# A two-layer decoder on one core: layer 0's experts with the products of tokens and gates first in each part of a step, rotary on DVE, and more buffers for gated tokens in the last steps

## The chip, the cores and the metric

The kernel runs on one core of a Trainium2 chip. A core has five engines with a queue of instructions each: TensorE (PE, matmuls and transposes; its weight loads are shown apart as PEld), VectorE (DVE), ScalarE (ACT), GpSimd (POOL) and SyncE (SP), from which nearly all DMAs of the stage concerned are issued. An engine takes its instructions in order; one that waits holds up all behind it. The metric is the device time of one execution in microseconds (us). Of the kernel before, the median of three runs is 3584.25 us (3584.22 to 3586.48).

## The reference, cut to what matters

The whole computation is two decoder layers on x of 32 sequences of 100 tokens with 256 features, each layer with self-attention, cross-attention and a feed-forward part. The change touches only layer 0's feed-forward part, which is itself an attention with rotary followed by a choice of two experts out of eight. It gets the layer norm of x, and its result is added to x:

```python
q_in = _apply_rope(xh, sin, cos).reshape(B, S, E)   # r1 = x1*cos - x2*sin; r2 = x1*sin + x2*cos
q = (q_in @ Wq.T + bq).reshape(B, S, H, D)          # H = 16 heads of D = 16
k = (q_in @ Wk.T + bk).reshape(B, S, H, D)
v = (x @ Wv.T + bv).reshape(B, S, H, D)
...                                                 # causal attention, softmax
attn_out = ctx @ out_proj_w.T + out_proj_b
x1 = _layer_norm(x + attn_out, ln1_w, ln1_b)
gates = softmax(x1 @ gate_w.T + gate_b)             # 8 experts
_, top_idx = top_k(gates, 2)
expert_outputs = einsum('bsd,efd->bsef', x1, expert_w) + expert_b
...                                                 # the two chosen, times their gates, summed
return _layer_norm(x1 + moe_out, ln2_w, ln2_b)
```

Here S is 100, E (the width) is 256, and an expert is one 256x256 matrix with a bias.

## The kernel before, in words

**Tiling.** The 32 sequences form 8 groups of 4 (G = 4, NG = 8); a group has 400 tokens (GT), which stand either as rows (100 partitions, 4 sequences, 256 features) or turned (128 partitions, 2 halves of the features, 400 tokens). All is float32.

**The experts** are computed densely. A token's gate for an expert is zero unless the expert is one of its two. `gating(g, part)` (L985) makes the gates of group g: part 0 turns the rows x1 into x1T and multiplies by the gate weights; part 1 turns the logits back and takes exponentials; part 2 normalises and selects the top two (`top2`, L887), a chain of some twenty short DVE operations that ends in `wt`. `gates_turned` (L1026) turns `wt` on PE and stores it in DRAM; `gate(n)` (L1043) loads row n of it, broadcast to 128 partitions, into `wb` (three buffers), n counting group and expert, 0 to 63. `gated(n)` (L1053) multiplies the group's x1T by `wb` on DVE, one 128x800 product at L1056, into `xg` (two buffers). `experts(g, i, m)` (L1059) multiplies the gated tokens of experts 2i and 2i + 1 by the half m of their matrices on PE (L1068, each float32 matmul is two in the trace), the sum over experts running in PSUM for two and in `acc` on DVE for all (L1074); for i = 0 the biases are added on PE (L1063). `end(g, part)` (L1080) turns `acc` back (L1090), takes its layer norm, and adds it to x with three POOL operations (L1102 to L1104).

**The attention** (`heads_attention`, L275) is shared with layer 0's self-attention; the part that the change touches is its loop over steps. Here a step s is one sequence, g = s // 4 + 1 and i = s % 4. With 32 sequences there are 42 steps, 0 to 41; from step 32 on no attention work is left but the last output. `norm(g, part)` (L928) prepares a group: part 0 statistics on DVE (`stats`, L150, with its power on POOL at L174), part 1 scaling on ACT (L192), part 2 turns it on PE (L943), copies it on ACT (L946, `xlT`) and applies rotary: a product with cosines (L953, DVE for groups 0 and 1, POOL after), two products with sines on POOL (L955, `xwT`) and their sum on POOL (L958, `xrT`). `queries_or_keys` reads xrT, `values` reads xlT.

**The order** of PE, DVE, ACT and POOL is the program's own in this stage (`in_order`); buffers are handed out by the planner, and an instruction waits for the last reader of its buffer. In a step DVE's order is: `masked(s + 1, 0)` (L365), statistics of `norm` at i = 1, `fill(s, 0)`, `divided(s - 1)` (L423, L425), `lowered(s + 1, 0)` (L376, whose subtraction L377 is POOL's), `masked(s + 1, 1)`, `fill(s, 1)`, `lowered(s + 1, 1)`, `values` (L343), `fill(s, 2)`, `output(s - 1)` (L965), `fill(s, 3)`. PE's order is scores (L356), queries and keys (L223), the transposes of `norm`, `fill(s, 0)`, `divided` (L418), `turn_weights` (L389), `fill(s, 1)`, values, `turn_sums` (L431), `sums` (L405), `fill(s, 2)`, `output`, `fill(s, 3)`. PSUM has two double banks for scores and four single ones (`mm_tile`) for all else.

`fill(s, part)` (L1106) places the experts' work between the parts of a step. With 4i + part as the place in a group's four steps: `rows_of` (attention's residual and its layer norm) at 3, 4 and 6, `gating` at 9, 10 and 12, `gates_turned` at 14, all for the group before; `end` at i = 1. With n = 2(s - 9), `experts` for n and n + 1 stands in parts 1 and 2, and after all else comes the product n + 1 in part 0 and n + 2 in part 3, each followed by the load three ahead.

Of the kernel before, what the change touches and what calls it, by code (L numbers as in the profile page):

```python
# [10 lines left out]
F32 = mybir.dt.float32  # L11
# [4 lines left out]
ALU = mybir.AluOpType  # L16
AX = mybir.AxisListType

P = 128
B, T, D = 32, 100, 256  # L20
S2, DC = 361, 192
G = 4
NG = B // G
GT = G * T
H = 16
XH = 4
E = 8
# [39 lines left out]
def kernel(ctx: ExitStack, tc: tile.TileContext, io: dict, out: bass.AP):  # L67
    nc = tc.nc
# [49 lines left out]
    def bc(ap, axis, n):  # L118

        ap = ap.unsqueeze(axis)  # L120
        shape = list(ap.shape)
        shape[axis] = n
        return ap.to_broadcast(shape)
# [151 lines left out]
    def heads_attention(pool, w, wo, bias, norm, turn, res, fill):  # L275
# [87 lines left out]
        def masked(s, hf, ps):  # L363
            sm = pool.tile([T, 8, T], F32, tag="s", name="s", bufs=3)
            nc.vector.tensor_tensor(  # L365
                sm.rearrange("p (r j) k -> p r j k", r=2),
                ps[:T, :, :GT].rearrange("p r (j k) -> p r j k", k=T),
                bc(bc(causal, 1, 4), 1, 2), ALU.add,
            )
            sms[s, hf] = sm  # L370
# [74 lines left out]
            res(s, ps[:T, :D])  # L445

        with in_order():
            for part in range(3):
                norm(0, part)
            turned_[0] = turn(0)  # L450
            for m in range(4):
                queries_or_keys(0, m)
            values(0)
            ps = scores(0)
            for hf in range(2):
                masked(0, hf, ps[hf])
                lowered(0, hf)
                exponentials(0, hf)
            for part in range(3):
                norm(1, part)  # L460
            for s in range(B + 1 + fill.steps):
                g, i = s // G + 1, s % G
                more = s + 1 < B
                if more:
                    ps = scores(s + 1)
                    masked(s + 1, 0, ps[0])
                if g < NG:
                    if i == 0:
                        turned_[g] = turn(g)
                    for m in ((0,), (1,), (2, 3), ())[i]:  # L470
                        queries_or_keys(g, m)
                if i >= 1 and g + 1 < NG:
                    norm(g + 1, i - 1)
                fill(s, 0)
                if 1 <= s <= B:
                    divided(s - 1)
                if more:
                    lowered(s + 1, 0)
                    masked(s + 1, 1, ps[1])
                if s < B:  # L480
                    turn_weights(s)
                fill(s, 1)
                if more:
                    lowered(s + 1, 1)
                    values(s + 1)
                if 1 <= s <= B:
                    turn_sums(s - 1)
                if more:
                    exponentials(s + 1, 0)
                if s < B:  # L490
                    sums(s)
                fill(s, 2)
                if 1 <= s <= B:
                    output(s - 1)
                if more:
                    exponentials(s + 1, 1)
                fill(s, 3)
# [47 lines left out]
    rope = plain(w2, "rope", [P, 3, T])  # L545
    kch = CCH + [(S2, T)]
    NK = S2 + T
    with tc.tile_pool(name="x0", bufs=2) as pool, tc.tile_pool(name="x0p", bufs=1) as fixed:
# [288 lines left out]
        with in_order():  # L837
# [11 lines left out]
            for n in range(-4, B + 1):  # L849
# [14 lines left out]
                g = (n + 4) // G + 1  # L864
                if (n + 4) % G == 3 and g < NG:
                    lnTs[g] = latents_turned(lns.pop(g))
                g = (n + 5) // G
# [55 lines left out]
    with tc.tile_pool(name="f0", bufs=2) as pool:  # L923
# [4 lines left out]
        def norm(g, part):  # L928


            if part == 0:
                xls[g] = stats(xs[g], G, tag="n", shift=True)
            elif part == 1:
                xl = pool.tile([T, G, D], F32, tag="xl", name="xl", bufs=3)
                scaled(xl, xs[g], G, xls[g])
                xls[g] = xl
            else:
                xl2 = xls[g].rearrange("p g (d two) -> p g d two", two=2)
                xlT = xlTs[g] = pool.tile([P, 2, GT], F32, tag="xlT", name="xlT")
                for c in range(2):  # L940
                    ps = mm_tile()
                    for i in range(G):
                        nc.tensor.transpose(  # L943
                            ps[:, i * T : (i + 1) * T], xl2[:, i, :, c], ident[:T, :T]
                        )
                    nc.scalar.copy(xlT[:, c, :], ps[:, :GT])  # L946
                xrT = xrTs[g] = pool.tile([P, 2, GT], F32, tag="xrT", name="xrT")
                xwT = pool.tile([P, 2, GT], F32, tag="xwT", name="xwT", bufs=1)
                l4, r4, w4 = (
                    x.rearrange("p c (i t) -> p c i t", t=T) for x in (xlT, xrT, xwT)  # L950
                )
                first = nc.vector if g < 2 else nc.gpsimd
                first.tensor_tensor(r4, l4, bc(bc(rope[:, 0], 1, G), 1, 2), ALU.mult)  # L953
                for c in range(2):
                    nc.gpsimd.tensor_tensor(  # L955
                        w4[:, c], l4[:, 1 - c], bc(rope[:, 1 + c], 1, G), ALU.mult
                    )
                nc.gpsimd.tensor_tensor(xrT, xrT, xwT, ALU.add)  # L958

        def turn_group(g):  # L960
            return xrTs.pop(g), xlTs.pop(g)
# [81 lines left out]
        def gate(n):  # L1043

            if n < E * NG:
                g, e = n // E, n % E
                wb = pool.tile([P, GT], F32, tag="wb", name="wb", bufs=3)
                nc.sync.dma_start(
                    wb, wt_dram[g : g + 1, e * GT : (e + 1) * GT].to_broadcast([P, GT])
                )  # L1050
                wbs[n] = wb

        def gated(n):  # L1053
            if n < E * NG:
                xg = pool.tile([P, 2, GT], F32, tag="xg", name="xg")
                nc.vector.tensor_tensor(xg, x1Ts[n // E], bc(wbs.pop(n), 1, 2), ALU.mult)  # L1056
                xgs[n] = xg

# [47 lines left out]
        def fill(s, part):  # L1106

            g, i = s // G, s % G
            if 1 <= g <= NG:
                for at, f, *args in (  # L1110
                    (3, rows_of, 0), (4, rows_of, 1), (6, rows_of, 2), (9, gating, 0),
                    (10, gating, 1), (12, gating, 2), (14, gates_turned),
                ):
                    if 4 * i + part == at:
                        f(g - 1, *args)
                        if at == 14:
                            for n in range(3 if g == 1 else 1):
                                gate(E * (g - 1) + n)
            if 3 <= g and i == 1 and part in (0, 1, 3):
                end(g - 3, part)  # L1120


            n = 2 * (s - 2 * G - 1)
            if part in (1, 2) and 0 <= n < E * NG:
                experts(n // E, n % E // 2, part - 1)
            n += part // 3 + 1
            if part % 3 == 0 and 0 <= n < E * NG:
                gated(n)
                if n % E != 5:
                    gate(n + 3)  # L1130

        fill.steps = 2 * G + 1
        heads_attention(
# [311 lines left out]
    gated = {}  # L1445
# [840 lines left out]
```

## Time and profile before

| what | us |
|---|---|
| median of three runs | 3584.25 |
| the profiled execution | 3584.9 |
| its span | 3583.1 |
| PE busy | 3363.2 (94%) |
| DVE busy | 1863.4 (52%) |
| ACT busy | 1601.8 (45%) |
| POOL busy | 1287.8 (36%) |
| in 760 to 1365: PE, DVE, ACT, POOL busy | 509.43, 365.77, 235.41, 255.49 |
| L1056, products of tokens and gates, 64 | 69.1 (1089 ns each) |
| L953, L955, L958, rotary on POOL | 11.4, 17.7, 15.1 |
| L1068, experts' matmuls, 512 | 202.1 |

Times inside the execution are in us from the span's start. A row of the timeline gives start, duration, engine, line, operation, output and inputs, shape and count; in brackets stands how long the engine had been idle before and what ended that. Rows merge neighbours of one kind, so a row with x8 lasts from the first start to the last end. PE's clock is shown as a share of full speed.

### The profile page before, as it was taken

To read this page: it belongs to the slowest core of one execution; us is meant where nothing else is said; L and a number is where in the kernel's file an instruction comes from. 1 tells how busy PE (TensorE), PEld (TensorE's weight loads), DVE (VectorE), ACT (ScalarE), POOL (GpSimd) and SP (SyncE) were. 2 spreads that over 40 slices of the span, in tenths; PEclk is the share of its full clock that TensorE was granted. 3 is DMA by queue.
4 is the path that set the end of the run, shared out by engine and by line. 5 is a ranking of instruction groups with operands and counts; after the bars stand their busy time and mean duration, and the time that the engine had idled before them with its cause. 6 is when DMAs were issued, how large, how long until landed. Compare 5 with 4: busy or idle time off the path is not lost. (4 is left out here: it accounts for less than half of the span.)

```text
span 3583.1 us, 66359 instructions
## 1 busy us (share of the span) xinstructions
PE 3363.2 (94%) x25978; PEld 2261.1 (63%) x25978; DVE 1863.4 (52%) x5298; ACT 1601.8 (45%) x3533; POOL 1287.8 (36%) x947
## 2 busy tenths in 40 slices
PE   7998999968889977999999999999999999999997
PEld 5775666646556633333466666666666668899997
DVE  6777777636666644755455564555646552011111
ACT  4664666645434413566554544445444442211111
POOL 3445887855444421011133323333333332012221
PEclk9999999989999998999999999999999999999999
DMA  3002101000111111000100000000000003456665
GB/s 83 2 2 63 26 22 23 16 17 11 26 22 28 28 37 49 1 1 1 41 9 23 19 20 24 20 25 22 20 19 26 20 17 105 128 184 186 183 185 145
DMA packets 109218, 168.15 MB, mean 47 GB/s; under 512 B 14996, under 2 KB 89628, under 8 KB 108444
## 3 DMA queue, kind: packets, MB, share of 16 engines
q1 hardware_dynamic: 94238, 145.60, 13.6%
q0 software_dynamic: 12688, 15.36, 2.2%
q8 instruction: 207, 3.39, 0.4%
q10 hardware_dynamic: 1982, 2.95, 0.2%
q14 instruction: 103, 0.84, 0.1%
HBM read 138.32 MB, written 28.82 MB: 47 GB/s over the span
## 5 line engine op out<-in xcount | busy, mean ns | idle before, releaser
L1678 POOL TENSOR_TENSOR ex<-ex,rc 100x1444 f32<-100x1444 f32 x128 | 331.8, 2592 | 784.1 <-DVE rc L1677 742.8
L1669 ACT ACTIVATE ex<-s,nmx 100x361 f32<-100x361 f32 x512 | 303.2, 594 | 143.5 <-DVE nmx L1660 143.5
L377 POOL TENSOR_TENSOR s<-s,nmx 100x800 f32<-100x800 f32 x128 | 194.7, 1522 | 282.5 <-DVE nmx L376 206.3
L1276 ACT ACTIVATE h<-sc,cols 128x800 f32<-128x800 f32 x256 | 222.0, 924 | 134.9 <-PE sc L1270 134.5
L1660 DVE CUSTOM_DVE_ANT_0 s<-sc,mb 100x361 f32<-100x361 f32 x512 | 250.6, 527 | 7.6 <-PE sc L1653 7.6
L2133 POOL DMA_INDIRECT acc_dram<-y,xg x57 | 89.0, 1562 | 451.2 <-DVE y L2132 213.7
L1068 PE MATMUL mm<-xg,f_we 128*128 128x400 f32 x512 | 202.1, 537 | 39.6 <-DVE xg L1056 37.9
L2115 ACT ACTIVATE hgT<-sc 128x1024 f32<-128x1024 f32 x57 | 58.3, 1023 | 351.3 <-PE sc L223 351.3
L223 PE MATMUL sc<-xgT,w1b 128*128 128x128 f32 x1824 | 213.1, 275 | 0.4 <-DMA w1b<-in_f_w 0.4
L223 PEld LDWEIGHTS sc<-xgT,w1b 128*128 128x128 f32 x1824 | 208.3, 192 | 0.7 <-issue 0.6
L2132 DVE TENSOR_SCALAR y<-mm,gx 128x256 f32<-128x256 f32 x57 | 27.6, 484 | 348.1 <-PE mm L223 348.1
L223 PE MATMUL mm<-wx,hgT 128*128 x912 | 206.1, 380 | 0.0
L1653 PE MATMUL sc<-kT,qT 64*100 64x361 f32 x1024 | 197.8, 463 | 0.0
L1625 PE MATMUL mm<-x_wa,cT 128*128 128x512 f32 (+1 forms) x512 | 191.0, 496 | 0.1
L1685 PE MATMUL mm<-ident,ex 100*128 100x100 f32 (+1 forms) x1536 | 168.7, 258 | 18.7 <-ACT kT L1607 9.7
L174 POOL TENSOR_TENSOR rs<-va,neghalf 100x4 f32<-100x4 f32 (+1 forms) x96 | 97.5, 1018 | 237.1 <-DVE va L170 120.7
L223 PEld LDWEIGHTS mm<-wx,hgT 128*128 128x128 f32 x912 | 169.2, 190 | 20.5
L1703 PEld LDWEIGHTS mm<-eT,vb 128*64 128x64 f32 (+1 forms) x3072 | 136.8, 137 | 67.3 <-issue 66.4
L1595 PE MATMUL mm<-cT,x_wa 128*128 128x361 f32 x512 | 177.9, 470 | 0.7 <-DVE lnT L148 0.7
L1068 PEld LDWEIGHTS mm<-xg,f_we 128*128 128x128 f32 x512 | 96.5, 199 | 123.1 <-DVE xg L1056 46.1
L1685 PEld LDWEIGHTS mm<-ident,ex 100*128 100x128 f32 (+1 forms) x1536 | 143.1, 152 | 39.8 <-ACT kT L1607 13.9
L1692 ACT COPY eT<-mm 128x400 f32<-128x400 f32 (+1 forms) x256 | 125.6, 491 | 89.9 <-PE mm L1685 88.5
(347 smaller groups left out, 7323.6 us busy)
## 6 DMA issues: line engine op xcount, KB each, us to landing
w1b<-in_f_w SPq DMA_DIRECT2D x57, 1024.0 KB
wb<-wt_dram SPq DMA_DIRECT2D x64, 200.0 KB
wx<-in_f_w SPq DMA_DIRECT2D x8, 1024.0 KB
xg<-sorted_dram SPq DMA_DIRECT2D x57, 132.5 KB
cb<-in_ctx SPq DMA_DIRECT2D x32, 192.0 KB
cT<-in_ctxT SPq DMA_DIRECT2D x32, 180.5 KB
cT<-in_ctxT SPq DMA_DIRECT2D x64, 90.2 KB
x<-in_x SPq DMA_DIRECT2D x8, 400.0 KB
```

Source lines behind the costliest of these rows:

```text
L223: nc.tensor.matmul(ps, lhsT[k], rhs[k], start=(k == 0), stop=(k == n - 1))
L377: nc.gpsimd.tensor_tensor(sm, sm, bc(nmx, 2, T), ALU.add)
L1068: nc.tensor.matmul(ps[:, :GT], f0_we[:, k, e * D + m * P : e * D + (m + 1) * P], xgs[E * g + e][:, k, :], start=(i > 0 and e == 2 * i and ...
L1276: nc.scalar.activation(h1, both[r2][:, :, :GT], AF.Tanh, bias=col("a1_b1", o))
L1595: nc.tensor.matmul(kTs[u][c][:, :S2], x1_wa[:, m * P : (m + 1) * P], cT[:, 0, :], start=True, stop=False,)
L1625: nc.tensor.matmul(ps[e][:kn, :n], cT[:, 0, at], x1_wa[:, 1024 + c0 : 1024 + c0 + n], start=True, stop=False,)
L1653: nc.tensor.matmul(ps[:T, e, :S2], qT[p0 : p0 + 64, m, tok], kT[p0 : p0 + 64, c, :], start=True, stop=True,)
L1660: nc.vector.tensor_tensor_reduce(s[:, e, :], ps[:T, e, :S2], mb, 1.0, 3.4e38, ALU.add, ALU.min, nmx[:, e : e + 1],)
L1669: nc.scalar.activation(ex[:, 2 * c + e, :], s[:, e, :], AF.Exp, bias=nmx[:, e : e + 1], scale=-1.0, accum_out=sm[:, 2 * c + e : 2 * c + e ...
L1678: nc.gpsimd.tensor_tensor(ex, ex, bc(rc, 2, S2), ALU.mult)
L1685: nc.tensor.transpose(pt[:kn, j * T : (j + 1) * T], ex[:, j, k0 : k0 + kn], ident[:T, :T])
L1703: nc.tensor.matmul(po[64 * e : 64 * e + 64, m * T : (m + 1) * T], vb[k][:kn, v0 + 64 * h : v0 + 64 * h + 64] if k < 2 else vb[2 + u % 2][: ...
```

## The change

- `norm` gets a part 3: the rotary, taken out of part 2. All its four operations are on DVE, for every group. It is called after part 2 for groups 0 and 1, and for the others in the step with i = 3, after `masked(s + 1, 1)` and ahead of `turn_weights(s)`.
- In `fill`, the products stand first in parts 0 and 3, ahead of `rows_of`, `gating` and `end`. How far they go is counted: up to n + 1 in part 0 and n + 2 in part 3, as before; from step 32 on two more; until step 36 not past the last product of group 6 (number 55).
- The third part of `gating` (normalising and the top two) moves from place 12 (i = 3, part 0) to place 11 (i = 2, part 3).
- From product 48 on `xg` takes its buffers from the tags `xg`, `xlT` and `xrT` in turn, two products each: six buffers of one size.
- Loads of gates are issued in order by `gates()`, up to three ahead of the products made and as far as the gates have been stored.

```diff
@@ heads_attention
-            for part in range(3):
+            for part in range(4):
                 norm(0, part)
...
-            for part in range(3):
+            for part in range(4):
                 norm(1, part)
...
                     masked(s + 1, 1, ps[1])
+                if i == 3 and g + 1 < NG:
+                    norm(g + 1, 3)
                 if s < B:
                     turn_weights(s)
@@ norm
-            else:
+            elif part == 2:
                 xl2 = xls[g].rearrange("p g (d two) -> p g d two", two=2)
...
+            if part == 3:
+                xlT = xlTs[g]
                 xrT = xrTs[g] = pool.tile([P, 2, GT], F32, tag="xrT", name="xrT")
...
-                first = nc.vector if g < 2 else nc.gpsimd
-                first.tensor_tensor(r4, l4, bc(bc(rope[:, 0], 1, G), 1, 2), ALU.mult)
+                nc.vector.tensor_tensor(r4, l4, bc(bc(rope[:, 0], 1, G), 1, 2), ALU.mult)
                 for c in range(2):
-                    nc.gpsimd.tensor_tensor(
+                    nc.vector.tensor_tensor(
                         w4[:, c], l4[:, 1 - c], bc(rope[:, 1 + c], 1, G), ALU.mult
                     )
-                nc.gpsimd.tensor_tensor(xrT, xrT, xwT, ALU.add)
+                nc.vector.tensor_tensor(xrT, xrT, xwT, ALU.add)
@@ gated
-                xg = pool.tile([P, 2, GT], F32, tag="xg", name="xg")
+                tag = "xg" if n < 2 * (B - 2 * G) else ("xg", "xlT", "xrT")[(n // 2 + 1) % 3]
+                xg = pool.tile([P, 2, GT], F32, tag=tag, name="xg")
@@ fill
+            n = 2 * (s - 2 * G - 1)
+            if part % 3 == 0:
+                upto = n + part // 3 + 1
+                if s >= B:
+                    upto += 2
+                if s < B + G:
+                    upto = min(upto, E * (NG - 1) - 1)
+                while done[0] <= min(upto, loads[0] - 1):
+                    gated(done[0])
+                    done[0] += 1
+                    gates()
...
-                    (10, gating, 1), (12, gating, 2), (14, gates_turned),
+                    (10, gating, 1), (11, gating, 2), (14, gates_turned),
...
                         if at == 14:
-                            for n in range(3 if g == 1 else 1):
-                                gate(E * (g - 1) + n)
+                            stored[0] = E * g
+                            gates()
...
-            n += part // 3 + 1
-            if part % 3 == 0 and 0 <= n < E * NG:
-                gated(n)
-                if n % E != 5:
-                    gate(n + 3)
+
+        done, loads, stored = [0], [0], [0]
+
+        def gates():
+            while loads[0] < min(done[0] + 3, stored[0]):
+                gate(loads[0])
+                loads[0] += 1
```

More of the change, by code (lines that the diff above doesn't have):

```diff
@@ L1116, in fill @@
                         if at == 14:
-                            for n in range(3 if g == 1 else 1):
-                                gate(E * (g - 1) + n)
+                            stored[0] = E * g
+                            gates()
             if 3 <= g and i == 1 and part in (0, 1, 3):
                 end(g - 3, part)
-            n = 2 * (s - 2 * G - 1)
             if part in (1, 2) and 0 <= n < E * NG:
                 experts(n // E, n % E // 2, part - 1)
-            n += part // 3 + 1
-            if part % 3 == 0 and 0 <= n < E * NG:
-                gated(n)
-                if n % E != 5:
-                    gate(n + 3)
+        done, loads, stored = [0], [0], [0]
[3 more added lines that the diff above has]
+                loads[0] += 1
         fill.steps = 2 * G + 1
```

## The prediction

> **What bounds the kernel now.** I read the page first (PE 94% busy over the span), then busy times by stretch, which place the stage that the change touches: it begins near 760 us and its last transposes end at 1358. This answer is busy time of each engine per 40 us (PE, PEld, DVE, ACT, POOL), then PE's granted clock and DMA:
>
> ```profile
> 840.00:880.00 40.00, 31.81 (x357) 22.90 (x356) 27.24 (x68) 21.07 (x43) 20.17 (x22) 0.86 0.01 2
> 1160.00:1200.00 40.00, 38.32 (x322) 24.91 (x320) 27.23 (x67) 18.42 (x37) 20.46 (x16) 1.00 0.14 27
> 1280.00:1320.00 40.00, 30.47 (x77) 14.86 (x78) 17.19 (x46) 6.12 (x12) 9.93 (x7) 0.80 0.13 31
> ```
>
> PE is the bound in the middle, with DVE at two thirds; at the ends PE idles and its clock falls. So I listed PE's waits (total us, times, longest) in 760 to 1365:
>
> ```profile
> PE mm L1068 <- DVE xg L1056: 37.9, 16, 4.3
> PE mm L223 <- POOL xrT L958: 10.1, 3, 5.4
> ```
>
> Nearly all of PE's recoverable idle time is the wait for gated tokens. The timeline shows why, at step 11:
>
> ```profile
> 930.07 1.97 DVE L898 TENSOR_TENSOR hot<-rows,idf 100x32 f32<-100x32 f32 x2
> 932.07 1.87 POOL L958 TENSOR_TENSOR xrT<-xrT,xwT 128x800 f32<-128x800 f32 x1
> 932.07 1.91 DVE L1022 TENSOR_TENSOR wt<-hot 100x32 f32<-100x32 f32 x1
> 934.13 0.98 DVE L1056 TENSOR_TENSOR xg<-x1T,wb 128x800 f32<-128x800 f32 x1
> 935.16 3.03 PE L1068 MATMUL mm<-xg,f_we 128*128 128x400 f32 x4 [4.31 <-DVE xg L1056]
> ```
>
> The top-2 selection stands ahead of the product, and its small operations last as long as POOL's rotary operations beside them. At step 27, where no rotary is left:
>
> ```profile
> 1200.05 0.29 DVE L898 TENSOR_TENSOR hot<-rows,idf 100x32 f32<-100x32 f32 x2
> 1200.38 0.19 DVE L1022 TENSOR_TENSOR wt<-hot 100x32 f32<-100x32 f32 x1
> 1201.75 1.61 PE L1068 MATMUL mm<-xg,f_we 128*128 128x400 f32 x4 [1.78 <-DVE xg L1056]
> ```
>
> Same selection, 3.4 us shorter; the wait is 1.78, and the four matmuls take 1.61, not 3.03: after the long wait PE was at half clock. The last steps look like this:
>
> ```profile
> 1342.26 0.57 DVE L1074 TENSOR_TENSOR acc<-mm,acc 128x400 f32<-128x400 f32 x1 [2.11 <-PE mm L1068]
> 1342.75 1.88 DVE L1056 TENSOR_TENSOR xg<-x1T,wb 128x800 f32<-128x800 f32 x2
> 1343.79 5.64 PE L1068 MATMUL mm<-xg,f_we 128*128 128x400 f32 x16 [1.57 <-DVE xg L1056]
> ```
>
> PE and DVE take turns: with two buffers the next products can't start before PE is done with the last.
>
> [...]the 0.29 us pair takes 1.97 beside POOL.[...] Here waits over 4 us are followed by half-rate matmuls (3.03 for 1.61) and waits of 1.8 and 1.9 us are not; but 2.25 us at 1309.18, soon after another, is.[...]
>
> **The change, part by part.**
>
> *Rotary to DVE.* DVE gains per group two 128x400 products and a 128x800 sum, and from group 2 on the 128x800 product: 0.99 (its own row, L953 on DVE), twice 0.57, 0.98: 3.1 us. No row has a 128x400 with both operands in SBUF; 0.50 (half of 0.99) to 0.57 (the PSUM form, L1074) bound it, I take 0.57. That is 22.7 us on DVE in eight groups and 44.2 off POOL (11.4 + 17.7 + 15.1). For groups 0 and 1 the chain is bare, PE waits 5.42 and 3.85: POOL needed 4.8 us from turned tokens to xrT (769.35 to 774.15), DVE needs 3.1: saved 1.7 twice, **3.4**. At step 3 POOL's rotary holds back L377, so exponentials and PE (0.85, 1.15, 0.92): the first stays, the rest goes, with some clock: **2.5** (0 to 2.9).
>
> In a step with i = 3 the rotary now stands between the second mask and `turn_weights` in program order, after `divided`. Behind it on DVE wait the sum L1074, which frees a PSUM bank, the second maximum L376 (POOL's L377, ACT's exponential) and the values L343. At step 11, counting from 925.83: product to 926.8, top-2 to 929.8, mask 930.7, product 931.7, reciprocal and division 932.3, maximum 933.2, mask 934.1; [...]the rotary runs to 937.6 (start to start 2.8), sum 938.1, maximum 939.0, values 939.4. PE, with 1.1 us of wait, is through this step's experts at 938.6, wants the sum's bank then (free at 938.1), the values' bank at 940.4 and the exponentials (941.5) about 942.9. The cover is 0.5 us at the tightest; gone, each us of lateness would cost one.
>
> *Top-2 one part earlier.* DVE does the same work before the second product in either order: product, mask, top-2, product or product, top-2, mask, product. So this alone gains nothing; the gain is that POOL's rotary is no longer beside it. Steps 11, 15, 19, 23: waits of 4.31, 4.28, 4.13, 4.12 become 1.1 each (931.7 against PE ready at 930.6), 12.4 us. Half clock: 1.42 on the four matmuls, 0.88 on the values, 0.4 on what follows, 2.7 a time; half of that at step 23: 9.5. Together **21.9**. Step 7: the same selection delays the division, PE waits 4.42 (L431 at 877.94) and then runs slow (1.56 for 0.89, 1.76 for 1.03): the division moves from 877.8 to 873.8, PE wants it at 873.5: 4.1 + 3.1 = **7.2**. Steps 27 and 31 (1.78, 1.91): nothing.
>
> *Products first.* At i = 1 the product overtakes the statistics of `rows_of` (2.4 us): 0.91 at step 9, 0.80 at step 29, some 0.1 between: **2.0**. The statistics come one product (0.95) later, and ACT's scaling two parts on has room for that; the division doesn't move, both stood ahead of it. Each product is followed by one broadcast load, the same 64 in the same order; SP's queue holds only these and eight stores, so none is moved past another.
>
> *Six buffers, last steps.* From output(31) at 1272.14 to the last transpose at 1358.27 are 86.1 us. PE's work there: eight steps of experts at 5.5 (16 matmuls, 5.64 less the overlap), 44.0; biases 4 x 0.86; transposes and gating 0.9 + 0.9 + 1.24 + 0.85 + 1.45 + 0.3 + 0.9; output 0.86: 54.8. Waits left: group 7's own chain. L965 at 1273.6, POOL's sum 3.0[...], statistics 2.4, power 1.2, ACT 2.07: PE is there 0.9 us early; L148 stands behind two products: 1.8; top-2 behind a product: 2.0 before L1030; L1090 twice 0.6: together 5.9. So 60.7 us, 25.4 saved; three products instead of two ahead of the division at step 32 cost 0.5, a half-clock spell after such a wait about 1: **24.0**. Broadcasts: store to load issue is 1.4 us (1313.75 to 1315.18), three loads are down some 5 us after issue; group 7's first product isn't needed before step 37, one step of 5.5 us later than its load can land.
>
> Sum 3.4 + 2.5 + 21.9 + 7.2 + 2.0 + 24.0 = 61.0. The profiled execution took 3584.9 (span 3583.1 and 1.8 around it): 3523.9. The median of the runs is 0.65 lower, so 3523. What follows the stage starts as much earlier; no wait in it is for a fixed time.
>
> **Rivals.** (1) DVE becomes the bound at i = 3: half a us of cover isn't there, the sum's bank is late by some 2 us and half clock stays in steps 11 to 23. Then of 24.4 (steps 3 to 23, less step 7) about 5 is left: 3543.[...] Against: the count above. (2) The last steps gain half:[...] 3535. Against: one step of look-ahead is longer than that. (3) Slower: [...]the second exponentials arrive late and PE's `turn_weights` stalls at half clock, in all six steps of groups 2 to 7. It must eat 61 us and 7 more to be seen: over 11 us a step, where DVE's rotary and one L377 are 4.6 together. It would need every such step's delay to be handed on to the next two. (4) The products don't go ahead: the extra buffers are only taken from product 48 on, and if a slot of `xlT` or `xrT` were still held, the last steps would be as now: 3547. The last reader of `xlT` is values(31) at step 30, product 48 comes at step 32; unlikely.
>
> **How the numbers follow.** 0.2% is 7.2 us, about what a measurement tells from no change. The forecast 0.70 (own range 3513 to 3534: [...]4 for half-clock spells, 4 for the last steps), rival 1 0.11, rival 2 0.10, rival 4 0.03, slower 0.04, no change 0.02. Range 3511 to 3546: 0.70 less its own tail of 0.08, with most of rivals 1 and 2. Faster 0.94, same 0.02, slower 0.04.
>
> **What would show it.** PE's wait for L1056 falls from 37.9 us to under 12; the `hot` pair takes 0.3 everywhere; xrT is ready 3.1 us after xlT in groups 0 and 1; no POOL rotary; DVE near 1870 us busy (1863.4 + 22.7[...]); steps 37 to 40 run at 5.5 us. I am wrong if L1068, L389 or L223 wait for L1074 or the exponentials at i = 3, if half clock stays there, or if the stage shrinks and a later one grows.

## The result, and the profile after

| | before | after |
|---|---|---|
| median, us | 3584.23 (3582.7 to 3586.48, 6 runs) | 3557.18 (3556.24 to 3562.76, 6 runs) |
| span of the profiled execution | 3583.1 | 3554.4 |
| PE, DVE, ACT, POOL busy | 3363.2, 1863.4, 1601.8, 1287.8 | 3353.6, 1873.7, 1602.8, 1258.7 |

The changed kernel takes 0.9925 of the time (95% interval 0.9915 to 0.9936), 27 us less. The forecast was 61 us less, 3523 with a range of 3511 to 3546: the sign was right, the size was not, and the measurement lies above the range.

Busy time by stretch, after (length, then PE, PEld, DVE, ACT and POOL busy, PE's granted clock, DMA):

```profile
840.00:880.00 40.00, 33.32 (x408) 24.45 (x407) 29.16 (x75) 22.18 (x45) 16.68 (x17) 0.96 0.01 2
1280.00:1320.00 40.00, 37.55 (x117) 20.36 (x116) 24.26 (x53) 3.86 (x8) 11.68 (x7) 0.95 0.14 42
```

The last steps improved most (PE 37.55 of 40 for 30.47). PE's waits from 755 to 1335, after (total us, times, longest):

```profile
PE mm L1073 <- ACT back L410: 11.2, 4, 2.8
...
PE mm L1073 <- DVE xg L1061: 8.1, 7, 1.9
PE mm L223 <- DVE xrT L961: 7.2, 3, 3.6
```

The line numbers moved: L1073 is the experts' matmul (L1068 before), L1061 the product (L1056), L961 the rotary's last sum (L958). The wait for gated tokens fell from 37.9 us in 16 waits to 8.1 in 7. At the top stands a wait that wasn't there before: four times 2.8 us for `back`, ACT's copy of the attention's sums (L410). It means that PE has no PSUM bank: the experts' second half gets the bank that `back` still has to be copied out of. The timeline of step 11, after, shows what holds `back` up:

```profile
926.96 0.98 DVE L365 TENSOR_TENSOR s<-sc,causal 100x800 f32<-100x800 f32 x1
927.19 4.00 POOL L377 TENSOR_TENSOR s<-s,nmx 100x800 f32<-100x800 f32 x1 [10.48 <-DVE nmx L376]
927.86 0.98 DVE L956 TENSOR_TENSOR xrT<-xlT,rope 128x800 f32<-128x800 f32 x1
928.76 1.05 DVE L958 TENSOR_TENSOR xwT<-xlT,rope 128x400 f32<-128x400 f32 x2
929.84 2.19 DVE L961 TENSOR_TENSOR xrT<-xrT,xwT 128x800 f32<-128x800 f32 x1
931.22 0.87 ACT L382 ACTIVATE ex<-s 100x800 f32<-100x800 f32 x1 [2.63 <-POOL s L377]
932.00 0.47 ACT L410 COPY back<-mm 128x400 f32<-128x400 f32 x1
932.52 4.54 PE L1073 MATMUL mm<-xg,f_we 128*128 128x400 f32 x8 [2.81 <-ACT back L410]
```

Read it from below. PE waits 2.81 us for `back` and then runs in part at half clock (4.54 us for eight matmuls that take 2.95 in experiment 1; the granted clock over them is 0.64). `back` stands on ACT behind the first exponential (L382), which waits for POOL's L377: the sums that `back` copies were ready at 929.06, where PE's L405 ended, and it starts at 932.00. L377 is recorded as starting at 927.19, 0.67 us before the rotary, and takes 1.52 in experiments 1 and 9; here it takes 4.00 and ends at 931.19, 1.35 after the recorded start of the rotary's last operation, which lasts 2.19 for 0.98. The rotary's three products meanwhile last 0.98 and, the two together, 1.05, as they do in groups 0 and 1 with no L377 beside them (0.99 and 1.05). My estimate from these rows: L377's last 1.52 us begin at 929.67, about where the products end (929.81), so that it ran behind the products and the sum behind it. The same holds in all six steps with a rotary: L377 starts 0.67 to 0.74 us ahead of it and takes 4.00 to 4.07.

In the last steps the alternation of PE and DVE is gone, but three places are left, of which these rows show two (the third, 1.89 us for `wt`, was in the forecast):

```profile
1255.33 0.99 DVE L1061 TENSOR_TENSOR xg<-x1T,wb 128x800 f32<-128x800 f32 x1 [1.17 <-DMA wb<-wt_dram]
...
1257.00 0.39 PE L431 MATMUL mm<-ident,o 100*128 100x100 f32 x2 [1.58 <-DVE o L425]
...
1273.22 2.07 ACT L192 ACTIVATE yo<-yo,sh,rs 100x256 f32<-100x256 f32 x4 [1.84 <-POOL sh L176]
1275.20 0.67 ACT L139 ACTIVATE x1T<-mm,cols 128x400 f32<-128x400 f32 x1
...
1275.92 3.03 PE L223 MATMUL mm<-x1T,f_wg 128*128 128x400 f32 x4 [3.83 <-ACT x1T L139]
...
1307.16 19.07 PE L1073 MATMUL mm<-xg,f_we 128*128 128x400 f32 x56
```

At step 32 the third product of the three waits for its load, and the division behind it on DVE is late. At step 34 ACT's copy of x1T stands behind the scaling of `yo`, PE waits 3.83 us and falls to half clock (granted 0.50; 3.03 us for four matmuls that took 1.61 at 1201.75 of the kernel before, granted 1.00). From 1307 on the matmuls follow each other with no wait, as forecast.

**Where the time went, step by step.** PE's product of `oT` with `f_wo`, the start of each output, marks the steps. Differences of the marks, us (the last line ends with the last transposes):

| stretch | before | after | saved | forecast |
|---|---|---|---|---|
| span's start to output(0) | 814.25 | 811.70 | 2.55 | 3.4 |
| to output(4), rotary of step 3 in it | 37.07 | 39.03 | -1.96 | 2.5 |
| output(4) to (7), step 7 in it | 38.16 | 33.81 | 4.35 | 7.2 |
| to outputs 8, 12, 16, 20, 24, 28 (i = 1) | 96.73 | 93.74 | 2.99 | 2.0 |
| to outputs 10, 14, 18, 22 (steps 11 to 23) | 79.97 | 73.74 | 6.23 | 21.9 |
| to output(31), step 32 | 8.18 | 9.98 | -1.80 | part of 24.0 |
| output(31) to the last transposes | 86.13 | 67.93 | 18.20 | with the line above 24.0 |

With 0.16 lost in the other stretches the sum is 30.4 us. After the stage 1.7 us are lost again; nothing of the change is there, and no run tells where from. Single executions of one kernel differ by more than that (3538.33 to 3545.39 in experiment 12), and the profile is of one: no edit below changes an instruction ahead of the stage, yet its first transposes (L943, later L945) start anywhere from 763.95 us (experiment 12) to 770.40 (experiment 2), at 766.47 before and 767.85 after. So the first line of the table holds 1.38 us lost ahead of the stage and 3.93 saved in it.

### The profile page after: what moved, and what is told of

Same layout as the page of the kernel before. It is cut to its first block, busy times and chain, and to the rows that moved or that the text cites. A ratio compares the mean times of both kernels' runs of the same rounds, so it can differ in the third digit from the quotient of the medians.

```text
span 3554.4 us, 66360 instructions
## 1 busy us (share of the span) xinstructions
PE 3353.6 (94%) x25978; PEld 2256.7 (63%) x25978; DVE 1873.7 (53%) x5328; ACT 1602.8 (45%) x3533; POOL 1258.7 (35%) x917
## 3 DMA queue, kind: packets, MB, share of 16 engines
q10 hardware_dynamic: 1982, 2.95, 0.2%
## 5 line engine op out<-in xcount | busy, mean ns | idle before, releaser
L377 POOL TENSOR_TENSOR s<-s,nmx 100x800 f32<-100x800 f32 x128 | 210.1, 1641 | 332.4 <-DVE nmx L376 251.1
L1073 PE MATMUL mm<-xg,f_we 128*128 128x400 f32 x512 | 195.2, 527 | 19.3 <-ACT back L410 11.2
L1721 PE MATMUL mm<-eT,vb 128*64 128x100 f32 (+1 forms) x3072 | 162.3, 254 | 0.0
```

What stands on the lines that cost most here:

```text
L377: nc.gpsimd.tensor_tensor(sm, sm, bc(nmx, 2, T), ALU.add)
L1073: nc.tensor.matmul(ps[:, :GT], f0_we[:, k, e * D + m * P : e * D + (m + 1) * P], xgs[E * g + e][:, k, :], start=(i > 0 and e == 2 * i and ...
L1721: nc.tensor.matmul(po[64 * e : 64 * e + 64, m * T : (m + 1) * T], vb[k][:kn, v0 + 64 * h : v0 + 64 * h + 64] if k < 2 else vb[2 + u % 2][: ...
```

## The experiments

Each was compared with the kernel before on the same chip, where its median was between 3583.77 and 3586.98 us, so that ratios are the safer thing to compare; rows are from one execution each. The edits are to the changed kernel unless it is said otherwise. "Steps 11 to 23" is the stretch to outputs 10, 14, 18 and 22: 79.97 us before, 73.74 after.

**1. The rotary behind the values.**

```diff
-                if i == 3 and g + 1 < NG:
-                    norm(g + 1, 3)
                 if s < B:
                     turn_weights(s)
                 fill(s, 1)
                 if more:
                     lowered(s + 1, 1)
                     values(s + 1)
+                if i == 3 and g + 1 < NG:
+                    norm(g + 1, 3)
```

> The rotary of groups 2 to 7 stays on DVE but moves behind `values(s + 1)`, so that the division, both masks, both maxima and the values are ahead of it. Theory A ([...]L377 takes 4.0 us for 1.5, the first exponential and `back` behind it on ACT are late, and PE waits 2.81 us for `back`'s PSUM bank in steps 11, 15, 19, 23 and then runs at half clock): these four waits vanish and 4 x (2.8 + about 2.5) = 21 us are saved, with 3 to 5 more at steps 3 and 7: 3531 to 3537 against 3557 for the change. The long L377 is then the second half's, which nobody needs before the next step. Theory B (the 22.7 us added to DVE are what holds PE, wherever they stand): within 6 us of 3557, PE's waits moved to another bank or to the products.

Measured 3546.23 (3544.45 to 3548.76), ratio 0.9895 (0.9878 to 0.9911). Rows of step 11:

```profile
924.08 1.52 POOL L377 TENSOR_TENSOR s<-s,nmx 100x800 f32<-100x800 f32 x1 [10.48 <-DVE nmx L376]
...
926.35 3.44 POOL L377 TENSOR_TENSOR s<-s,nmx 100x800 f32<-100x800 f32 x1 [0.74 <-DVE nmx L376]
926.41 0.47 ACT L410 COPY back<-mm 128x400 f32<-128x400 f32 x1
926.54 2.95 PE L1073 MATMUL mm<-xg,f_we 128*128 128x400 f32 x8
```

The first L377 is back at 1.52, `back` is copied in time, PE doesn't wait and stays at full rate (2.95 us for the eight matmuls). Now the second L377 meets the rotary (3.44), and nothing waits for that. Steps 11 to 23 take 56.47 us, 17.3 less than in the changed kernel and 23.5 less than before: the place of the rotary was what cost the main term of the forecast. But the kernel gained 11 us only. The steps after these show where some of it went: outputs 9, 17, 29 and 30 come 20.36, 20.44, 19.50 and 13.97 us after their forerunners, for 18.76, 18.76, 16.52 and 12.36, with the same waits and half-rate matmuls after them. That is taken up below. The time lies between the two forecasts: theory A had the waits right and the total 9 to 15 us too low.

**2. `back` ahead of the first exponential,** in this stage alone (the one with a `bias`).

```diff
-                if more:
+                if bias is None and more:
                     exponentials(s + 1, 0)
                 if s < B:
                     sums(s)
+                if bias is not None and more:
+                    exponentials(s + 1, 0)
```

> The rotary stays where the change put it; in this stage ACT copies the weighted sums (`back`) ahead of the first half's exponential instead of behind it. Theory A: [...]`back` no longer stands behind it, so PE's wait for the bank in steps 11 to 23 goes: 15 to 21 us saved, 3536 to 3542. Theory B: no more than 5 us. If [...]the late second exponential is what counts, PE waits at L389 in the next step instead and less than half is saved.

Measured 3549.21 (3545.22 to 3553.65), ratio 0.9898 (0.9882 to 0.9915). The wait for `back` is gone with the rotary where the change put it and L377 still slow (4.00 us): steps 11 to 23 take 57.04 us. So it is `back` behind the exponential, not the exponential itself, that PE missed. The forecast of 3536 to 3542 was missed by the same kind of long stretches (output(17) 20.45, output(29) 19.55).

**3. Rotary back on POOL, all else as changed.** The four operations of groups 2 to 7 and the last three of groups 0 and 1, at the place they had before.

> The rotary of groups 2 to 7 is back on POOL in part 0 (and its last three operations of groups 0 and 1 too), all else as in the change. Theory A: the top-2 selection now starts some 2 us earlier than POOL's rotary[...]: a wait of 2 to 4 us for the product in steps 11 to 23; the last steps keep their gain: 3558 to 3568. Theory B: DVE is relieved of 22.7 us, PE's wait for the bank goes and nothing takes its place: under 3545.

Measured 3570.94 (3569.36 to 3571.33), ratio 0.9960 (0.9946 to 0.9975), 3 us above theory A: with the rest of the change in place, putting the rotary back on POOL costs half of the gain. PE's waits:

```profile
PE mm L1074 <- DVE xg L1062: 25.0, 7, 5.2
```

Steps 11 to 23 take 83.20 us, more than before the change: the selection, a part earlier, stands ahead of the step's second product, and its small operations still last as long as POOL's rotary beside them: at 930.98 one on `wt` takes 1.91 us beside POOL's 1.87, for 0.19 at 926.38 in experiment 4, with no POOL operation beside it.

**4. The selection back at place 12, all else as changed.**

```diff
-                    (10, gating, 1), (11, gating, 2), (14, gates_turned),
+                    (10, gating, 1), (12, gating, 2), (14, gates_turned),
```

> The changed kernel with the top-2 selection back at place 12 (i = 3, part 0), all else as changed. The prediction's step: its place alone gains nothing: 3555 to 3559. Rival (what counts is not the product but what stands behind the selection on DVE: division, maximum, POOL's subtraction, the first exponential, `back`): in the steps with i = 3 these are 2 to 3 us later, PE's wait for `back` grows from 2.8 to 4 to 6 us, and the wait of 0.83 for the product goes: four to six steps at 1.5 to 3 us: 3562 to 3575.

Measured 3561.26 (3560.54 to 3562.32), ratio 0.9935 (0.9918 to 0.9952), 4 us slower by the medians than with the early selection (the intervals overlap, but steps 11 to 23 are longer too, 76.61 us), just short of what the rival said and outside of what the forecast's step said. PE's first row of waits shows the term:

```profile
PE mm L1073 <- ACT back L410: 15.6, 4, 3.9
```

The product goes ahead of the selection, but division, maximum, L377 and `back` come later. In steps 27 and 31, where there is no rotary, the late place is the better one: output(26) follows in 12.94 us for 14.12, output(30) in 11.65 for 12.36.

**5. Products first alone, on the kernel before.** The block of the product and its load moved to the top of `fill`, nothing else.

> The kernel before with one part of the change alone: the products stand first in parts 0 and 3 of `fill`, as far as before and with the same loads behind them; rotary, selection and buffers as before. The prediction's step gives this 2.0 us, in the steps with i = 1: 3580 to 3583.5. Rival (in the last steps the order of the products is worth the 8 us that the changed kernel without products ahead kept there): 3573 to 3578, with output(31) to the last transposes at 78 us for 86.1.

Measured 3565.96 (3565.12 to 3570.1), ratio 0.9947 (0.9931 to 0.9964): 20 us from what the forecast priced at 2.0, and more than the rival gave it. Step 11 of this kernel:

```profile
926.13 0.98 DVE L1056 TENSOR_TENSOR xg<-x1T,wb 128x800 f32<-128x800 f32 x1
...
930.90 1.97 DVE L898 TENSOR_TENSOR hot<-rows,idf 100x32 f32<-100x32 f32 x2
...
934.10 0.36 PE L431 MATMUL mm<-ident,o 100*128 100x100 f32 x2 [2.54 <-DVE o L425]
```

With the product in front of the selection the wait of 4.31 for it is gone, though beside POOL's rotary the `hot` pair still lasts 1.97 (0.29 at step 27 of the kernel before); what is late is the division, by 2.54. Steps 11 to 23 take 69.15 us. From output(31) to the last transposes it is 79.2 us for 86.1: at step 33 the product no longer stands behind the statistics, where it made PE wait 3.76 us before.

With this run there are four kernels that all have the products first and differ, up to step 31, only in where the rotary and the selection stand. Steps 11 to 23 take:

| | selection late (place 12) | selection early (place 11) |
|---|---|---|
| rotary on POOL | 69.15 (experiment 5) | 83.20 (experiment 3) |
| rotary on DVE, ahead of `turn_weights` | 76.61 (experiment 4) | 73.74 (changed kernel) |

With the products first the old places of rotary and selection are the best of the four: each of the two moves alone makes these steps longer, and both together still by 4.6 us. Only once PE no longer waits for what stands behind L377 (56.47, 57.04 and 57.88 us, experiments 1, 2 and 9) is the rotary better on DVE.

**6. No products ahead, two buffers throughout.**

```diff
-                tag = "xg" if n < 2 * (B - 2 * G) else ("xg", "xlT", "xrT")[(n // 2 + 1) % 3]
+                tag = "xg"
@@ fill
-                if s >= B:
-                    upto += 2
```

> The change without the two products more from step 32 on and with two buffers throughout. The forecast had 24 us for this part; by the two traces it is 16 to 18: 3573 to 3576. If the last steps are bound by something else, 3560 to 3565.

Measured 3564.94 (3559.78 to 3566.4), ratio 0.9943 (0.9927 to 0.9960): products ahead are worth 8 us, half of the 16 to 18 that were expected of them. From output(31) to the last transposes it is 77.8 us, so 8.3 of the 18.2 saved there come without them, from the order.

**7. The two places of the last steps.**

```diff
-                if s >= B:
+                if s > B or (s == B and part == 3):
                     upto += 2
@@
-            if 3 <= g and i == 1 and part in (0, 1, 3):
+            if 3 <= g and i == 1 and part in (0, 1):
                 end(g - 3, part)
+            if 3 <= g and part == 3 and i == (3 if g == NG else 1):
+                end(g - 3, part)
```

> The changed kernel with the two edits of the last steps alone. Theory (the division at step 32 is late by a product that waits for its load, and x1T by the scaling of `yo`): the wait of the turn of o falls from 1.58 to under 0.3, that for x1T from 3.83 to 1.7, since DVE's half of x1T is ready at 1273.7, and the half-rate matmuls after it (3.03 and 3.73) go to full rate: 1.5 + 2.1 + 2.2 = 5.8 us, 3550 to 3553. Rival[...]: 3555 to 3559, with products of 3 us and more in steps 35 to 37.

Measured 3554.11 (3552.85 to 3556.97), ratio 0.9913 (0.9896 to 0.9929). The median is 3 us lower, not 5.8, and the profiled execution doesn't show where: from output(30) to the last transposes it takes 79.55 us, where the changed kernel's takes 77.91. Rows of it:

```profile
1270.47 0.31 PE L210 MATMUL mm<-ident,x 100*128 100x100 f32 x1 [2.25 <-ACT x L192]
...
1293.86 5.74 DVE L1061 TENSOR_TENSOR xg<-x1T,wb 128x800 f32<-128x800 f32 x2 [0.39 <-DMA wb<-wt_dram]
...
1303.04 5.65 PE L1073 MATMUL mm<-xg,f_we 128*128 128x400 f32 x8
```

The wait of 1.58 for the division is gone, and so is that of 3.83 for x1T. But three products now stand together at step 32, POOL's sum `xl` beside them (L979) takes 4.83 us for 3.93, and PE waits 2.25 for `x`, where it waited 0.63; the matmuls after it still run at half rate (3.03 and 3.75). Later it is as the rival said: POOL's operations of `end`, now at step 35, make two products last 5.74 us for 1.89, PE waits 1.90 for the sum into `acc` behind them, and half rate follows (5.65 for 2.95).

**8. Edits 1, 2 and 7 together.**

> The rotary moved behind the values and `back` ahead of the first exponential (both as in the two runs that had one of them), and in the last steps: no products ahead in part 0 of step 32, and in group 8's steps the scaling of `yo` moved from i = 1 to i = 3, so that ACT's copy of x1T isn't behind it. Theory: the gains add up where they are in different steps. 3546.2 with the late rotary, less 1.6 for the division at step 32, less 2.1 for the wait for x1T and 2.2 for the half clock behind it; the second of the first two edits adds at most 1. So 3539 to 3543. Rival[...]: 3544 to 3550, with half-rate matmuls in places where the kernel with the late rotary has full rate.

Measured 3547.76 (3545.89 to 3551.65), ratio 0.9898 (0.9882 to 0.9915), as the rival had it: the gains don't add up. From output(30) to the last transposes it takes 77.99 us for 78.27 in experiment 1, so the edits of the last steps bring next to nothing there. Steps 11 to 23 are as short as in the first experiment, and its long stretches are all there too (outputs 9, 17, 29 and 30 in 20.41, 20.45, 19.55 and 13.96).

**9. A pause ahead of the rotary.** For groups 2 to 7 a useless maximum, one input, 0.56 us:

```diff
+                if g >= 2:
+                    nc.vector.tensor_reduce(
+                        small.tile([P, 1], F32, tag="gap", name="gap"), xlT[:, 0, :], AX.X, ALU.max
+                    )
                 nc.vector.tensor_tensor(r4, l4, bc(bc(rope[:, 0], 1, G), 1, 2), ALU.mult)
```

> The changed kernel with a useless DVE operation of one input (a maximum over 128x400, some 0.5 us) ahead of the rotary for groups 2 to 7. In the changed kernel POOL's L377 starts at 927.19 and the rotary at 927.86, yet L377 lasts 4.00. Theory S[...]: with the pause L377 lasts 1.5 to 1.7, the rotary's first product 1.2 to 1.6, PE's wait for `back` falls from 2.8 to under 0.7 and full clock stays: 3543 to 3550. Theory D[...]: L377 lasts 4 us and more, the wait for `back` is 2.8 to 3.4: 3556 to 3561.

Measured 3541.51 (3538.93 to 3543.01), ratio 0.9880 (0.9864 to 0.9897). Work was added, and 16 us are gained, 1.5 more than theory S allowed for. Step 11 (here L1077 is the experts' matmul, L960 the rotary's first product):

```profile
925.19 1.52 POOL L377 TENSOR_TENSOR s<-s,nmx 100x800 f32<-100x800 f32 x1 [10.47 <-DVE nmx L376]
925.86 0.56 DVE L957 TENSOR_REDUCE gap<-xlT 128x1 f32<-128x400 f32 x1
...
926.33 1.23 DVE L960 TENSOR_TENSOR xrT<-xlT,rope 128x800 f32<-128x800 f32 x1
...
927.52 0.47 ACT L410 COPY back<-mm 128x400 f32<-128x400 f32 x1
...
928.05 2.95 PE L1077 MATMUL mm<-xg,f_we 128*128 128x400 f32 x8 [0.33 <-ACT back L410]
```

L377 takes 1.52 again, the rotary's first product 1.23 for 0.98, PE waits 0.33 and stays at full rate (2.95); it is the same in all six steps (leads of 1.14 to 1.21 us). Steps 11 to 23 take 57.88 us, 22.1 less than before.

**10. The same pause between the first and the second product.**

> The changed kernel with the same useless maximum, but between the rotary's first product and its next two instead of ahead of the first. Theory[...]: L377 [...]ends about 1 us after the first product and lasts 2.3 to 2.8, the second product waits up to 0.5, the last sum is back at 1.0 and PE's wait for `back` about 1.2 to 1.7: 3546 to 3553. Rival[...]: L377 4.4 or more, the wait for `back` 3.2: 3556 to 3562.

Measured 3557.71 (3557.19 to 3559.57), ratio 0.9922 (0.9906 to 0.9939).

```profile
927.53 3.03 POOL L377 TENSOR_TENSOR s<-s,nmx 100x800 f32<-100x800 f32 x1 [10.48 <-DVE nmx L376]
...
929.10 0.56 DVE L958 TENSOR_REDUCE gap<-xlT 128x1 f32<-128x400 f32 x1
929.58 1.90 DVE L962 TENSOR_TENSOR xwT<-xlT,rope 128x400 f32<-128x400 f32 x2
```

L377 takes 3.03 us and ends at 930.56, 0.90 after the recorded end of the pause, and the two products behind the pause last 1.90 for 1.05. As an estimate from these rows, its last 1.52 us begin at 929.04, 0.06 ahead of the recorded start of the pause: here it ran ahead of two products and not only ahead of the sum. The wait for `back` falls to 1.8 and steps 11 to 23 to 70.72 us; the 3 us gained are lost again at outputs 29 and 30 (18.22 and 14.00 for 16.52 and 12.36), and the forecast of the time was wrong. The time is in the rival's range, but the rows show 3.03 us for L377 and a wait of 1.8, not the 4.4 or more and the 3.2 that it asked for.

**11. The second maximum as the pause.** `lowered(s + 1, 1)` ahead of the rotary in the steps with i = 3.

> The changed kernel with the second half's maximum (L376, 0.97 us, one input) ahead of the rotary in the steps with i = 3, in place of a useless operation: the same pause, made of work that has to be done anyway. Theory: the first L377 lasts 1.5 to 1.7, no wait for `back` over 0.5[...]. 3538 to 3544, as with the pause or a little better. Rival (the second exponential is late and PE waits for it, or for the values): 3546 to 3552.

Measured 3549.78 (3546.13 to 3553.02), ratio 0.9895 (0.9879 to 0.9912). At step 11 all is as with the pause: L377 1.52, PE's wait for `back` 0.33, full rate (2.95); steps 11 to 23 take 59.5 us. Against the pause the loss is outside of them: its output(0) is at 813.66, not 809.07, and outputs 9, 24, 25 and 29 are 1.7, 1.7, 0.9 and 1.5 us late. Nothing seen in the waits explains the steps. The late output(0) is no effect of the edit, which acts from step 3 on: in this execution the stage began at 769.41 us, in that of experiment 9 at 765.80. By the ratios the two kernels are 5 us apart, and their intervals overlap.

**12. The pause in groups 0 and 1 too, and there alone.**

> The kernel with the pause ahead of the rotary, with the pause also in groups 0 and 1, where it stands bare on the chain: 0.56 us twice. If times follow from waits alone: 3541.5 and 1.1, 3541.5 to 3544. If [...]a shift by half a us moves them: outside of that by 2 us or more, with the same waits and other matmuls at half rate.

> The changed kernel with the pause in groups 0 and 1 alone, the steps with i = 3 as changed. If times follow from waits alone: 3557.2 and 1.1, 3557 to 3560, with PE's waits for `back` at 2.8 as before. If half-clock spells move with a shift by half a us: outside of that by 2 us or more.

Measured 3542.49 (3538.33 to 3545.39), ratio 0.9887 (0.9870 to 0.9903), and 3556.56 (3555.64 to 3558.63), ratio 0.9924 (0.9907 to 0.9940). Both are within 1 us of the kernels that they were made from. They don't decide what they were meant to: PE's wait for group 0's `xrT` stays at 3.60, since the pause reads the half of xlT that is copied first and, as I estimate, is over about when the second half is there (in the changed kernel the copies end at 770.29 and 770.96, and the pause takes 0.56), so nothing was shifted. They do show that these two medians repeat within 1 us (single executions of the first spread over 7), and that one profile's long stretch can move: output(17) in 20.45 with the pause in groups 2 to 7, 18.76 here, where it is output(21) instead (20.11).

**13. The best version.** The pause of experiment 9, the first edit of experiment 7, and the selection at place 12 for groups 6 and 7.

> The kernel with the pause ahead of the rotary, and two edits read from the runs so far: no products ahead in part 0 of step 32 (output(31) then follows output(30) by 8.2 us for 10.0), and the top-2 selection of groups 6 and 7, whose steps have no rotary, back at place 12 (output(26) and output(30) follow their forerunners by 12.9 and 11.65 us there for 14.1 and 12.36). 3541.5 less 1.8, 1.2 and 0.7: 3536 to 3540. Rival[...]: anything from 3533 to 3546, with a step of 20.4 for 18.8 or 19.5 for 16.5 us that no wait accounts for.

Measured 3536.76 (3534.98 to 3540.1), ratio 0.9866 (0.9850 to 0.9883), within what was expected: output(26), (30) and (31) take 12.94, 11.65 and 8.18 us as read from the other runs. It is 20 us faster than the changed kernel.

**Half clock.** Two runs of the same code and the same wait, first the kernel of experiment 1, then that of experiment 9:

```profile
1212.27 3.03 PE L223 MATMUL mm<-x1T,f_wg 128*128 128x400 f32 x4 [1.08 <-DVE x1T L148]
```

```profile
1212.20 1.61 PE L223 MATMUL mm<-x1T,f_wg 128*128 128x400 f32 x4 [1.08 <-DVE x1T L148]
```

In both a wait of 1.40 us ended 1.3 us before this one began. One is followed by half rate (3.03 us), one isn't (1.61). The same is seen ahead of the stage, which no edit touches, in the kernel before and the changed one, after the same waits (2.59 and 2.60, then 1.29 us in both); the granted clock over these rows is 1.00 and 0.51:

```profile
752.34 1.80 PE L749 MATMUL sc<-kT,qT 64*100 64x461 f32 x8
```

```profile
751.50 3.40 PE L751 MATMUL sc<-kT,qT 64*100 64x461 f32 x8
```

By their lengths the four long stretches of experiment 1 cost 7.9 us, the one of experiment 9 costs 1.7; the medians differ by 4.7.

## Why the prediction was right and wrong

**Head (3.4).** Right: the two waits fell from 5.42 and 3.85 to 3.60 and 2.00, 3.67 together, and two 128x400 products take 1.05. From the stage's first transposes to output(0) 3.93 us are saved; only 2.55 shows at output(0), since those transposes start 1.38 us later, part of it from a half-rate row ahead of them (2.03 for 1.11, granted clock 0.50).

**Steps 11 to 23 (21.9, got 6.2).** The size was right, the claim that it would arrive was not: with the pause the same steps give 22.1. The step that failed is the order of the two: the forecast, by an estimate of mine, let the rotary wait for L377 and end at 937.6. It is L377 that was late, to 931.19 in the changed kernel, 4.00 us for 1.52. An earlier recorded start did not put it first: with 0.67 us of lead it took 4.00, with 1.14 (experiment 9, 925.19 against 926.33) it took 1.52. If it is the lead that decides between these two operations, the value lies between 0.74, the longest of the changed kernel, and 1.14. Why the earlier start is not enough, the rows don't tell. The second failure is in the list of what is queued behind: I looked at the sum's bank, the values and the exponentials, and left out `back`, which stands on ACT behind the first exponential and holds a bank. Experiment 2 shows that this link alone carries the cost: with L377 still at 4.00 us, steps 11 to 23 fall from 73.74 to 57.04.

**Rivals.** The first had the right place and nearly the right size (about 5 us left of 24.4, 3543; it was 4.3) with the wrong bank. The third set the rotary on DVE against L377 and asked for over 11 us a step; against the pause it costs 4 (18.58 us for 14.52 at step 11), which is why the sign didn't turn. The second had the last steps at half; they gave two thirds. What I had as alternatives came partly together, with step 3 and step 7 besides, and my range had allowed for one at a time.

**Top-2 one part earlier ("this alone gains nothing").** Wrong, and so is the sentence on DVE's order under it: with products first the late selection stands behind both products, the early one ahead of the second. Experiment 4 prices the early place at 4 us gained with the rotary on DVE, experiment 3 against experiment 5 shows it costing 14 us in steps 11 to 23 with the rotary on POOL.

**Products first (2.0, got 3.0 at i = 1).** The places counted were right. Missed was that this edit alone removes the wait of 4.31 at step 11, because place 12 is part 0. On the kernel before it is worth 20 us, 10.8 of them in steps 11 to 23: the rotary and the order were two cures of one wait, and I had given the wait to the rotary. So the 22.1 that the pause gives in these steps agree with the 21.9 forecast in the sum, but half of them come without the rotary.

**Steps 3 and 7 (2.5 and 7.2, got -2.0 and 4.4).** The old waits went, but of step 7's 4.42 for the division 1.65 is left, since the early selection still stands ahead of it. Beside that L377 and the rotary meet there too: L377 takes 4.00 at 827.00 and at 872.33. At step 3 PE then waits 1.57 for `xrT` and 1.82 for qT, where it waited 2.92 in all before; at step 7 it waits 1.25 for `back` and 1.45 for qT. The forecast had no price for a rotary that is on the path there.

**Last steps (24.0, got 16.4).** In the stretch of 67.9 us PE is busy 59.9, 5.1 more than counted; 3.9 of it is half clock (granted 0.92 over the stretch; 3.03 for 1.58, 3.73 for 2.95, 1.05 for 0.85, and 9.77 for 24 matmuls that take 8.33 in experiment 13), of which I had 1.0; the rest is work that I counted short. Idle are 8.0 for 5.9. The excess is the wait for x1T, 3.83: I had 1.8 for DVE's half of it (L148), and what came last was ACT's half, behind the scaling of `yo`. Step 32 cost 1.8 for 0.5, since the third product waits for its load.

**What held.** The wait for gated tokens under 12 us (8.1), DVE near 1870 (1873.7; the rotary's 22.7 are 22.9 by the forecast's own terms), steps 37 on without waits, no rotary on POOL. The sentence "I am wrong if ... half clock stays there" named the place where it was.

**Open.** Why the same waits are followed by half clock in one kernel and not in another, worth some 6 us between variants; and the 1.7 us after the stage.

## What to carry to other kernels

When two parts of a change could each remove one wait, price each alone and then the pair: here the cheap reordering alone was worth 20 us and the whole change 27, and moving the rotary on top of it made steps 11 to 23 longer until PE's wait behind L377 was removed. When work moves to DVE, look at which POOL operation is issued just ahead of it and who waits for that one, through to the PSUM bank at the end of the chain: here L377 went from 1.52 to 4.00 us, and PE waited 2.81 for the bank. A one-input operation on DVE between the two let this POOL operation through first. A useless one of 0.56 us did it (experiment 9, L377 back at 1.52); one that has to be done anyway did it as well (experiment 11, 1.52), but that kernel was no faster for it.

## What the runs showed of the hardware

A POOL operation that the trace shows as started ahead of DVE's can still be the one that is late: L377 with 0.67 us of lead took 4.00 us for 1.52, and with 1.14 us it took 1.52 while the DVE product took 1.23 for 0.98. By the estimates above, its last 1.52 us fell where a one-input operation of 0.56 us stood between the products (experiment 10, 3.03 us in all), or ahead of the rotary's sum (2.19 us for 0.98, though the rows show DVE idle for no more than 0.03 us there); in the six steps of the changed kernel they never fell between two products of the rotary that stood next to each other (4.00 to 4.07 us). And half clock did not go by one wait's length here: a wait of 2.81 us, and 1.40 and 1.08 close together, were followed by half-rate matmuls (4.54 for 2.95, and 3.03 for 1.61), the latter in some kernels and not in others, while one of 2.52 us in the kernel before (at 1334.96) was followed by four matmuls at full rate (1.58, granted clock 1.00). What it depends on, no run here shows.
